# A graph layer on one core: segment sums kept in PSUM banks by TensorE, register numbers in half of the partitions, and a new split of the gather

## The chip, the cores and the metric

The kernel runs on one core of a Trainium2 chip. The metric is the device time of one execution in microseconds. A core has TensorE (PE; matmuls), VectorE (DVE), ScalarE (ACT), GpSimd (POOL) and SyncE (SP); each takes its own instructions in order, and semaphores tie them together. DMAs are issued here by SP (plain ones) and by POOL (the indirect ones, which gather rows by an index).

## The reference, cut to what matters

There are 12,500 nodes with 48 features and 400,000 edges with 32 features, sorted by their target `dst`.

```python
h = jnp.maximum(_layernorm(x, axis=-1), 0.0)
x_i, x_j = h[dst], h[src]
tmp = jnp.concatenate([x_i, x_j, edge_attr], axis=1)      # 48 + 48 + 32
h = jax.nn.relu(tmp @ W1 + b1)                            # 128 hidden
msg = h @ W2 + b2
out = x + jax.ops.segment_sum(msg, dst, num_segments=12500)
```

## The kernel before, in words

First, `node_tables` makes two tables of the nodes: A (the target's part of `W1`, with the bias) and B (the source's part), each 12,500 rows of 128 numbers in HBM. B is kept in SBUF too, turned, as `bt`: one node is one column of 128 partitions. A check of the indices then chooses between `windows` and `general`; with this data it is `windows`, and all that follows is in it.

`windows` goes over 391 chunks of 1024 edges, that is 8 tiles of 128 edges. The edges are sorted by target, so the targets of a chunk lie in a window of W = 80 nodes. For a chunk c:

- `prepare(c)` (L421): SP loads the 80 rows of table A (`rhs`), the edge features (`lhs`) and the targets (`row`). POOL gathers rows of table B, one fetch per tile of 128 edges (L442); the fetches are spread by waits on VectorE's instructions seven chunks earlier. VectorE makes two one-hot matrices: L458 (window row by edge) and L464 (`hot`, edge by window column, from `wnum`, which lies in PSUM).
- `before(c)` (L476): per tile a matmul of `lhs` with `rhs` gives the target's and the edge's part of the hidden layer in the PSUM tile `pre`.
- Not all tiles get their B rows from POOL. Some get them **by columns**: VectorE and ScalarE copy single columns of `bt`, 128x1 each, into a tile `gt` (L384), with the column's address in a register, and TensorE turns it and adds it to `pre` (`turned`, L485). A few get them **by single rows**: SP issues one DMA of 512 bytes per edge (L416).
- `gathered` (L506, L504) adds the gathered rows to `pre`, and `hidden` (L513, L515) applies the relu.
- `fold(c)`: per tile `hid` times `hot` sums the hidden rows of each node of the window (L524), and `ones` times `hot` counts its edges (L529). Both go to the PSUM tile `p_g`, 128 x 2 x 80.
- `add(c)` (L543): VectorE adds `p_g` to a segment in SBUF, at the window's place in it (an address in a register).

Segments: 12 chunks (GQ) share a segment of L = 1024 nodes. There are two segment tiles, used in turn. At a segment's end `segment_next` clears the other tile (L559, two memsets) and copies the 80 nodes that go on (L561). `segment_sum` multiplies a segment by `W2` and the counts by `b2` in two blocks of 512 columns (L569, L570), and VectorE adds each to the piece of `x` that `segment_load` fetched (L571). `segment_store` writes it to the output (L575).

Numbers for registers: the host packs, per chunk, a row of the places of columns, row numbers, window starts and so on. The rows lie in the SBUF tile `last`, chunk c in partition c % 128. `numbers` (L345; the loads carry L349) emits a load of up to 32 of them into registers of one engine. `PARTS` says which engine copies how many columns: four VectorE parts of 19, 20, 16 and 16 columns and five ScalarE parts of 16, 151 in all, so `tiles_of` makes 458 tiles by columns. SINGLE = 12 single rows per chunk make 36 tiles by rows. POOL fetches the other 2631.

The order of the work is written out by hand in the loop at the end of `windows` (L577 to L622): iteration c prepares chunk c, computes `before`, `turned`, `gathered` and `hidden` of chunk c-1, and folds and adds chunk c-2. On VectorE an iteration is: L458, columns of part 0, L464, columns of part 1, (L571), L506, columns of part 2, L513, L515, L543, (L559, L561), columns of part 3. The load of a part's numbers stands directly ahead of the part's copies, but for part 0, whose copies follow L458 and whose load lies between the two, and part 3, whose load stands ahead of L543.

Of the kernel before, what the change touches and what calls it, by code (L numbers as in the profile page):

```python
# [16 lines left out]
P = 128  # L17
# [9 lines left out]
W = 80  # L27


GQ = 12  # L30
OFF = -(NCH - 3) % GQ
L = 1024
# [3 lines left out]
BLK = 512  # L36
STORE = 2
# [18 lines left out]
    (True, 0, 19, 1),  # L56
    (True, 19, 20, 20),
    (True, 39, 16, 40),
    (True, 55, 16, 56),
    (False, 71, 16, 72),  # L60
    (False, 87, 16, 88),
    (False, 103, 16, 104),
    (False, 119, 16, 120),
    (False, 135, 16, 136),
)
PART = sum(n for _, _, n, _ in PARTS)
BASE = 152
# [3 lines left out]
SEG0 = 130848  # L71
SEG_SIZE = 8 * L


SEG, NEXT, SEG2 = 153, 154, 155
PLACE0 = 156
SINGLE = 12
SINGLE_AT = 160
WIDTH = 172
SLOTS = (NCH + 2 + P - 1) // P  # L80
MOST = 32
# [197 lines left out]
def windows(nc, tc, gp, bt, ident, idx, x_t, tab_a, tab_b, dst, edge_t, w1, w2s, b2s, out_t):  # L279
# [3 lines left out]
    with ExitStack() as es:  # L283
        seg = es.enter_context(tc.tile_pool(name="segs", bufs=1))

        segs = [seg.tile([P, 2, L], F32, name=f"seg{k}") for k in range(2)]
# [6 lines left out]
        ps_g = es.enter_context(tc.tile_pool(name="ps_g", bufs=2, space=PSUM))  # L293
        ps_f = es.enter_context(tc.tile_pool(name="ps_f", bufs=1, space=PSUM))
        xp = es.enter_context(tc.tile_pool(name="xp", bufs=2))
        ps_w = es.enter_context(tc.tile_pool(name="ps_w", bufs=1, space=PSUM))


        wnum = ps_w.tile([P, W], F32, name="wnum")
# [16 lines left out]
        place = PARTS[0][3] - 1  # L316
        for a, b in ((place, SEG2), (NEXT, SEG)):
# [4 lines left out]
        at_place = slice(place, place + 1)  # L322
        nc.vector.scalar_tensor_tensor(
            last[:, :, at_place], last[:, :, at_place], 4.0, last[:, :, PLACE0 : PLACE0 + 1],
            op0=ALU.mult, op1=ALU.add,
        )
        for seg in segs:
            nc.vector.memset(seg, 0.0)
# [16 lines left out]
        def numbers(c, at, n, engine):  # L345

            got = []
            for k in range(0, n, MOST):
                got += nc.values_load_multi_w_load_instructions(  # L349
                    last[c % P : c % P + 1, c // P, at + k : at + min(k + MOST, n)],  # L350
                    engines=[engine], min_val=0, max_val=1 << 23,
# [9 lines left out]
        def load(c, part):  # L361
# [4 lines left out]
            if part == 0 and 2 <= c < NCH + 2:  # L366
                base, *nodes = numbers(c, at - 1, n + 1, engine)
                st[c - 2]["base"] = base
            else:
                nodes = numbers(c, at, n, engine) if n else []  # L370
# [590 lines left out]
```

## Time and profile before

| | us |
|---|---|
| median of 3 runs | 3562.99 (3554.6 to 3570.09) |
| the profiled execution | 3548.53 |
| its span, first to last instruction | 3546.7 |
| mean granted TensorE clock | 0.784 of full speed |

Reading the profile: a row of a group gives line, engine, operation, output and inputs, shapes and count, then the busy time, the mean of one in ns, and the engine's idle time ahead of it with what ended it. A row of a timeline gives start, duration, engine, line, operation and tiles; neighbours of one line are merged, with their count. Instructions of one engine overlap by some tens of ns, so a group's mean duration is longer than the distance from one start to the next. DVEq, ACTq, SPq and POOLq are the sequencers of the engines: loads of registers, waits and the issue of DMAs are theirs and are not counted as busy.

### The profile page before, as it was taken

To read this page: it belongs to the slowest core of one execution; us is meant where nothing else is said; L and a number is where in the kernel's file an instruction comes from. 1 tells how busy PE (TensorE), PEld (TensorE's weight loads), DVE (VectorE), ACT (ScalarE), POOL (GpSimd) and SP (SyncE) were. 2 spreads that over 40 slices of the span, in tenths; PEclk is the share of its full clock that TensorE was granted. 3 is DMA by queue.
4 is the path that set the end of the run, shared out by engine and by line. 5 is a ranking of instruction groups with operands and counts; after the bars stand their busy time and mean duration, and the time that the engine had idled before them with its cause. 6 is when DMAs were issued, how large, how long until landed. Compare 5 with 4: busy or idle time off the path is not lost.

```text
span 3546.7 us, 119948 instructions
## 1 busy us (share of the span) xinstructions
PE 2628.1 (74%) x17111; PEld 2359.2 (67%) x17111; DVE 3258.7 (92%) x30218; ACT 3123.8 (88%) x31115; POOL 2667.2 (75%) x2658
## 2 busy tenths in 40 slices
PE   8677677777777776777777777777777777777777
PEld 6566666667666766666667666666666666666666
DVE  6799999999999999999999999999999999999997
ACT  5898989899898898988999899998988899898884
POOL 5777777777777777777777777777777777777773
PEclk9677887786777778877787778777787788777777
DMA  5533333333333333333333333333333333333332
GB/s 201 164 97 99 96 93 94 93 93 102 95 93 92 95 90 103 95 96 93 92 95 97 97 96 96 95 92 93 99 95 93 95 91 93 103 96 94 91 95 58
DMA packets 197246, 349.05 MB, mean 98 GB/s; under 512 B 67763, under 2 KB 104517, under 8 KB 195157
## 3 DMA queue, kind: packets, MB, share of 16 engines
q0 software_dynamic: 84224, 172.62, 19.2%
q1 hardware_dynamic: 111952, 168.56, 15.8%
q14 instruction: 670, 5.48, 0.5%
q8 instruction: 140, 2.29, 0.3%
q10 hardware_dynamic: 260, 0.10, 0.0%
HBM read 321.55 MB, written 22.07 MB: 97 GB/s over the span
## 4 chain that ended last, share of the span: by engine, by line
DVE 68%; PE 8%; ACT 6%; issue 5%; DVEq 4%; DMA 3%; SPq 0%; ACTq 0%; POOL 0%; POOLq 0%
DVE gt L384 38%; DVE hid L506 8%; ACT gt L384 6%; DVE hot L464 6%; DVE lhs L458 5%; DVE hid L513 5%; DVEq L349 4%; PE p_g L524 4%; DMA gb<-tab_b,srci 3%; DVE seg L543 2%; DVE hid L515 2%; PE p_f L569 1%; PE p_f L570 1%; PE pre L476 1%; PE pre L485 1%
## 5 line engine op out<-in xcount | busy, mean ns | idle before, releaser
L384 ACT COPY gt<-bt 128x1 f32 x31040 | 3077.3, 187 | 334.0 <-PE pre L485 226.2
L442 POOL DMA_INDIRECT gb<-tab_b,srci x2631 | 2645.7, 1006 | 822.5 <-issue 371.7
L384 DVE COPY gt<-bt 128x1 f32 x27584 | 1818.8, 144 | 161.1 <-issue 104.3
L524 PE MATMUL p_g<-hot,hid 128*128 128x80 f32 x6250 | 1074.6, 344 | 873.8 <-DVE hid L513 873.4
L524 PEld LDWEIGHTS p_g<-hot,hid 128*128 128x128 f32 x6250 | 1004.6, 252 | 950.1 <-DVE hid L513 940.9
L476 PEld LDWEIGHTS pre<-rhs,lhs 112*128 112x128 f32 x6250 | 964.9, 243 | 86.1 <-issue 85.2
L476 PE MATMUL pre<-rhs,lhs 112*128 112x128 f32 x6250 | 994.1, 327 | 16.5 <-DMA lhs<-in_edge_t 16.3
L506 DVE TENSOR_TENSOR hid<-pre,gb 128x896 f32<-128x896 f32 (+2 forms) x391 | 408.7, 1045 | 0.6
L464 DVE TENSOR_TENSOR hot<-wnum,rel 128x640 f32<-128x640 f32 x391 | 318.2, 814 | 0.0
L458 DVE TENSOR_SCALAR lhs<-row,bw 80x1024 f32<-80x1024 int16 x391 | 290.2, 742 | 9.2 <-DMA row<-in_dst 9.2
L485 PE MATMUL pre<-ident,gt 128*128 128x128 f32 x916 | 270.2, 403 | 9.8 <-DVE gt L384 9.6
L513 DVE TENSOR_SCALAR hid<-hid 128x896 f32<-128x896 f32 (+2 forms) x391 | 243.0, 622 | 0.1
L529 PE MATMUL p_g<-hot,ones 128*128 128x80 bf16 x3125 | 239.4, 237 | 0.0
L529 PEld LDWEIGHTS <-ones 128*128 128x128 bf16 x3125 | 239.1, 132 | 0.0
L485 PEld LDWEIGHTS pre<-ident,gt 128*128 128x128 f32 x916 | 192.4, 269 | 11.2 <-issue 11.2
L543 DVE TENSOR_TENSOR seg<-seg,p_g 128x160 f32 x391 | 124.5, 318 | 15.1 <-issue 11.4
L515 DVE TENSOR_SCALAR hid<-pre 128x128 f32<-128x128 f32 (+1 forms) x389 | 118.7, 305 | 0.0
L569 PE MATMUL p_f<-seg,w2s 128*48 128x512 f32 (+1 forms) x134 | 106.5, 890 | 0.4 <-DVE seg L543 0.4
L571 DVE TENSOR_TENSOR xseg<-xseg,p_f 48x512 f32<-48x512 f32 (+1 forms) x67 | 45.0, 672 | 50.8 <-PE p_f L570 50.7
L570 PE MATMUL p_f<-seg,b2s 1*48 1x512 f32 (+1 forms) x134 | 86.6, 731 | 0.0
L570 PEld LDWEIGHTS p_f<-seg,b2s 1*48 1x48 f32 x134 | 12.4, 135 | 87.6 <-issue 87.6
L559 DVE MEMSET seg<- 128x944 f32 x64 | 54.1, 845 | 9.3
(67 smaller groups left out, 294.7 us busy)
## 6 DMA issues: line engine op xcount, KB each, us to landing
gr<-tab_b SPq DMA_DIRECT2D x4608, 0.5 KB
row<-in_dst SPq DMA_DIRECT2D x390, 160.0 KB
lhs<-in_edge_t SPq DMA_DIRECT2D x390, 128.0 KB
gb<-tab_b,srci POOLq DMA_INDIRECT x2631
rhs<-tab_a SPq DMA_DIRECT2D x391, 40.0 KB
xseg<-in_x_t SPq DMA_DIRECT2D x33, 192.0 KB
out_x<-xseg SPq DMA_DIRECT2D x33, 192.0 KB
tab_b<-tab SPq DMA_DIRECT2D x3, 1280.0 KB
```

Source lines behind the costliest of these rows:

```text
L384: done = copy(gts[of][:, e : e + 1], bt8[:, bass.ds(at, 4)].bitcast(F32))
L442: fetch = nc.gpsimd.indirect_dma_start(out=gb[:, t, :], out_offset=None, in_=tab_b[:, :], in_offset=bass.IndirectOffsetOnAxis(ap=srci[:, c ...
L458: mark(nc.vector.tensor_scalar(lhs[:W, : n * P], row[:, : n * P], bw[:, c : c + 1], None, op0=ALU.is_equal,), 0.8)
L464: mark(nc.vector.tensor_tensor(hot[:, :n, :], wnum.unsqueeze(1).to_broadcast([P, n, W]), rel[:, c * T : c * T + n].unsqueeze(2).to_broadca ...
L476: nc.tensor.matmul(pre[:, t, :], s["lhs"][:K, t * P : (t + 1) * P], s["rhs"][:K, :], start=True, stop=t not in turned_at(c),)
L485: nc.tensor.matmul(st[c]["pre"][:, t, :], gts.pop(j), ident, start=False, stop=True)
L506: mark(nc.vector.tensor_add(to, of, rows), 1.0)
L513: mark(nc.vector.tensor_scalar(of, of, 0.0, None, op0=ALU.max), 0.55)
L515: nc.vector.tensor_scalar(apart(c, s["h"], True), apart(c, s["pre"], True), 0.0, None, op0=ALU.max)
L524: nc.tensor.matmul(p_g[:, 0, :], s["h"][:, t, :], s["hot"][:, t, :], start=t == 0, stop=t == n - 1)
L529: nc.tensor.matmul(p_g[:, 1, :], ones, high[:, t, 1::2], start=t == 0, stop=t == n - 1)
L543: mark(nc.vector.tensor_add(to, to, s["p_g"]), 0.25)
```

## The change

The segment sums stay in PSUM. A segment is now 5 chunks (GQ) and L = 432 nodes, so that its sums fill most of one bank (`sums`) and its counts part of another (`degs`); two of each are used in turn. `segment_begin` clears both with a matmul of zeros. `fold` adds straight into them, at a place that TensorE takes from two registers (two numbers per chunk, loaded by TensorE). `add` and `segment_next` are gone, and with them L543, L559 and L561 and the clearing of the segments ahead of the loop. At the next segment's start ScalarE copies the sums and the first row of the counts to SBUF (`segment_copy`); one iteration later TensorE multiplies by `W2` and `b2` back into the bank of the sums (`segment_product`); one more later VectorE copies the 80 nodes that go on from the last segment's piece of the output and adds the product (`segment_sum`). The store comes two iterations after that. `wnum` now lies in the bank of the first `degs`.

The numbers for registers lie in 64 partitions, the lower 16 of each 32 (`row_of`), and `last` is longer for it. VectorE's parts are 16, 20, 20 and 20 columns, 156 with ScalarE's, which makes 474 tiles by columns; SINGLE is 16, which makes 48 tiles by rows; POOL fetches 2603. With `add` gone, the load of part 3 stands between L515 and the copies.

```diff
-GQ = 12
+GQ = 5
-L = 1024
+L = 432
-STORE = 2
+STORE = 4
 PARTS = (
-    (True, 0, 19, 1),
-    (True, 19, 20, 20),
-    (True, 39, 16, 40),
-    (True, 55, 16, 56),
+    (True, 0, 16, 0),
+    (True, 16, 20, 16),
+    (True, 36, 20, 36),
+    (True, 56, 20, 56),
...
-SINGLE = 12
+SINGLE = 16
+HALF_ROWS = 16
+USED = P // 2
+def row_of(c):
+    group, row = divmod(c % USED, HALF_ROWS)
+    return 2 * HALF_ROWS * group + row, c // USED
...
+        sums = [ps_s.tile([P, L], F32, name=f"sum{k}") for k in range(2)]
+        beside = ps_w.tile([P, L + W], F32, name="deg0")
+        degs = [beside[:, :L], ps_w.tile([P, L], F32, name="deg1")]
+        wnum = beside[:, L:]
...
-        for seg in segs:
-            nc.vector.memset(seg, 0.0)
...
+        def segment_begin(g):
+            for of in (sums[g % 2], degs[g % 2]):
+                nc.tensor.matmul(
+                    of, zeros[:, :P], zeros, start=True, stop=False, skip_group_check=True
+                )
         def fold(c):
...
+            for at, of, first in zip(
+                numbers(c, PLACE, 2, mybir.EngineType.PE), (sums[k], degs[k]),
+                (SUM0 + k * SUM_SIZE, DEG0 + k * SUM_SIZE),
+            ):
+                at = at.with_bounds(
+                    min_val=first, max_val=first + 4 * FAR, guaranteed_mod_val=0, out_of_modulus=4
+                ) - first
+                to.append(of.bitcast(U8)[:, bass.ds(at, 4 * W)].bitcast(F32))
             for t in range(n):
                 nc.tensor.matmul(
-                    p_g[:, 0, :], s["h"][:, t, :], s["hot"][:, t, :], start=t == 0, stop=t == n - 1
+                    to[0], s["h"][:, t, :], s["hot"][:, t, :], start=False, stop=False,
+                    skip_group_check=True,
                 )
...
-            mark(nc.vector.tensor_add(to, to, s["p_g"]), 0.25)
...
+        def segment_copy(g):
+            sm[g] = segp.tile([P, 2, L], F32, name="seg")
+            nc.scalar.copy(sm[g][:, 0, :], sums[g % 2])
+            nc.scalar.copy(sm[g][:1, 1, :], degs[g % 2][:1, :])
+        def out_of(g, n):
+            return sums[g % 2][:D, :n]
+        def segment_product(g, n):
+            seg, p_f = sm.pop(g), out_of(g, n)
+            nc.tensor.matmul(p_f, w2s, seg[:, 0, :n], start=True, stop=False, skip_group_check=True)
+            nc.tensor.matmul(
+                p_f, b2s[:1, :], seg[:1, 1, :n], start=False, stop=True, skip_group_check=True
+            )
+        def segment_sum(g, n):
             if g > 0:
...
+                of, = numbers(begin(g - 1), NEXT, 1, mybir.EngineType.DVE)
+                nc.vector.tensor_copy(
+                    xs[g][:, :W],
+                    xs[g - 1][:, bass.ds(of.with_bounds(min_val=0, max_val=FAR), W)],
+                )
+            nc.vector.tensor_add(xs[g][:, :n], xs[g][:, :n], out_of(g, n))
...
+                g, k = group(c - 2)
                 if 0 <= c - 2 < NCH:
+                    if c - 2 == begin(g):
+                        segment_begin(g)
                     fold(c - 2)
                 if 0 <= c - 1 < NCH:
                     turned(c - 1)
+                if g > 0 and k == 1:
+                    segment_product(g - 1, L)
+                if g > 0 and k == 2:
+                    segment_sum(g - 1, L)
                 if k == GQ - 3 or c == NCH - 1:
                     segment_load(g)
-                if g > 0 and k < L // BLK:
-                    segment_sum(g - 1, k, BLK)
                 if g > 0 and k == STORE:
                     segment_store(g - 1, L)
...
                 load(c, 3)
-                if 0 <= c - 2 < NCH:
-                    add(c - 2)
-                    if k == GQ - 1:
-                        segment_next(g)
                 columns(c, 3)
                 for part in range(DVE_PARTS, len(PARTS)):
                     load(c, part)
                     columns(c, part)
+                    if g > 0 and k == 0 and part == DVE_PARTS:
+                        segment_copy(g - 1)
```

More of the change, by code (lines that the diff above doesn't have):

```diff
@@ L365, in load @@
             engine = mybir.EngineType.DVE if dve else mybir.EngineType.Activation
[L366 to L370, printed above, removed]
-            regs[c, part] = nodes
+            regs[c, part] = numbers(c, at, n, engine) if n else []
         def columns(c, part):
@@ L907 @@
     by_tile = src.reshape(NT, P)
-    numbers = np.zeros((SLOTS * P, WIDTH), np.int32)
+    numbers = np.zeros((LAST * USED, WIDTH), np.int32)
     first = dst[::CE]
```

106 lines of the change are left out of this document (45 added, 61 removed).

## The prediction

> **What bounds the kernel now.** I read the page first, then the view of one line (L458, once per chunk), then the timeline of VectorE over one chunk, then SyncE's queue.
>
> ```profile
> PE 2628.1 (74%) x17111; PEld 2359.2 (67%) x17111; DVE 3258.7 (92%) x30218; ACT 3123.8 (88%) x31115; POOL 2667.2 (75%) x2658
> ...
> L384 ACT COPY gt<-bt 128x1 f32 x31040 | 3077.3, 187 | 334.0 <-PE pre L485 226.2
> L442 POOL DMA_INDIRECT gb<-tab_b,srci x2631 | 2645.7, 1006 | 822.5 <-issue 371.7
> L384 DVE COPY gt<-bt 128x1 f32 x27584 | 1818.8, 144 | 161.1 <-issue 104.3
> ```
>
> VectorE is the fullest. But POOL's 75% is a full engine as well: (2645.7 + 822.5) / 2631 = 1.32 us from fetch to fetch, and most of the idle part is 0.3 us of "issue" ahead of each. The next row gives the period.
>
> ```profile
> L458 DVE TENSOR_SCALAR lhs<-row,bw x391: 535/740/927, 104.4 to 3524.8; 80x1024 f32<-80x1024 int16 x195, 80x640 f32<-80x640 int16 x1
> ```
>
> (3524.8 - 104.4) / 390 = 8.77 us per chunk. One plain chunk on VectorE (timeline; start, us, engine, line), and three of its sequencer's loads of register numbers (one line's view; duration, then start):
>
> ```profile
> 2085.44 0.74 DVE L458 TENSOR_SCALAR lhs<-row,bw 80x1024 f32<-80x1024 int16 x1
> 2086.58 1.25 DVE L384 COPY gt<-bt 128x1 f32 x19 [0.40 <-issue]
> 2087.74 0.82 DVE L464 TENSOR_TENSOR hot<-wnum,rel 128x640 f32<-128x640 f32 x1
> 2088.64 1.31 DVE L384 COPY gt<-bt 128x1 f32 x20
> 2089.86 1.08 DVE L506 TENSOR_TENSOR hid<-pre,gb 128x896 f32<-128x896 f32 x1
> 2090.86 1.05 DVE L384 COPY gt<-bt 128x1 f32 x16
> 2091.83 0.61 DVE L513 TENSOR_SCALAR hid<-hid 128x896 f32<-128x896 f32 x1
> ...
> 2092.57 0.32 DVE L543 TENSOR_TENSOR seg<-seg,p_g 128x160 f32 x1
> 2092.80 1.05 DVE L384 COPY gt<-bt 128x1 f32 x16
> 2093.78 0.74 DVE L458 TENSOR_SCALAR lhs<-row,bw 80x1024 f32<-80x1024 int16 x1
> ```
>
> ```profile
> L349 DVEq TENSOR_LOAD <-last x1: 1101/1101/1101, 2089.6 to 2089.6; - x1
> L349 DVEq TENSOR_LOAD <-last x1: 1098/1098/1098, 2091.4 to 2091.4; - x1
> L349 DVEq TENSOR_LOAD <-last x1: 1348/1348/1348, 2093.2 to 2093.2; - x1
> ```
>
> Two things to see. A copy costs (2089.86 - 2088.64) / 20 = 0.061 us. And a load of 16 numbers takes 1.10 us, one of 20 numbers 1.35, so 0.062 us per number; the copies behind it start some 0.1 us after it has ended. It begins some 0.2 to 0.6 us ahead of the long operation in front of it (2093.2 against 2093.78, 2089.6 against 2089.86, 2091.4 against 2091.83), because the sequencer runs that far ahead, and it is free only as far as that operation covers it. The two loads of 20 stick out (after L458 and L464), the two of 16 just fit.
>
> **The change, VectorE.** (a) Five more copies: 5 x 0.061 = +0.31 us per chunk. (b) The load behind L458 falls from 20 numbers to 16: begun 0.55 us ahead, it ends 0.55 us after L458's start, under L458 itself. The first copy then comes 0.66 us after L458's start (0.74 less the overlap of 0.08 between neighbours, as in 2092.57 + 0.32 against 2092.80) instead of about 0.9, as after L464 here (1.14 after L458 in this chunk): -0.25. (c) The load behind L506 grows to 20: 2089.6 + 1.35 is 2090.95, the copies start near 2091.08 instead of 2090.86: +0.22. (d) L543 goes, 0.23 us. But the load behind L515 grows to 20 as well and has lost L543 as cover: 2091.4 + 1.35, and 0.1 to start, is 2092.8, where the copies start now. So the add's gain is eaten: 0. (e) Numbers in the lower 16 of each 32 partitions. The two rows are 8 chunks whose numbers lie in the lower half and 8 in the upper:
>
> ```profile
> L349 DVEq TENSOR_LOAD <-last x33: 1097/1346/1373, 2068.2 to 2134.8; - x33
> L349 DVEq TENSOR_LOAD <-last x33: 1122/1380/1395, 2489.8 to 2557.7; - x33
> ```
>
> 25 to 34 ns a load; three loads show, in half of the chunks: 0.03 x 3 / 2 = -0.05. Sum of (a) to (e): +0.23 us per plain chunk.
>
> A rule speaks against (b) to (d): the Trainium skill (DMA: Bandwidth & Descriptors, Latency and other measured facts) gives a register load a floor of about 600 ns, as if its size did not matter. By that, (c) and (d) would cost nothing. The rows above disagree: 16 and 20 numbers differ by 0.25 us.
>
> (f) The segment work. Now, every 12 chunks:
>
> ```profile
> 1942.88 0.32 DVE L543 TENSOR_TENSOR seg<-seg,p_g 128x160 f32 x1
> 1943.35 1.83 DVE L559 MEMSET seg<- 128x944 f32 x2
> 1945.10 0.18 DVE L561 COPY seg<-seg 128x160 f32 x1
> 1945.19 1.05 DVE L384 COPY gt<-bt 128x1 f32 x16
> ...
> 1950.38 0.67 DVE L571 TENSOR_TENSOR xseg<-xseg,p_f 48x512 f32<-48x512 f32 x1
> ```
>
> ```profile
> DVE xseg L571 <- PE p_f L570: 50.7, 36, 3.9
> ```
>
> From L543 to the copies 2.31 us instead of 0.23, two adds of 0.6, and 50.7 / 33 = 1.5 of waiting for the product: 4.8 us, 0.40 per chunk. Afterwards, every 5 chunks: a copy of 48x80 (at most the 0.18 above), an add of 432 columns (432/512 x 0.67 = 0.57), and one more register load, mostly under queued copies. That is 0.75 / 5 = 0.15. The product now stands one chunk ahead of its add, so its wait goes, though a late TensorE can delay L506 instead (third rival). Saving: 0.25.
>
> VectorE alone: +0.23 - 0.25, about -0.02 us per chunk, with 0.1 of doubt either way: no change. The two memsets ahead of the loop (L328) are 3.5 us that I leave in the doubt.
>
> **ScalarE and POOL.** ScalarE gets two copies of 432 columns per segment, of which there are 79: about 0.57 us each by L571's price, so 90 us in all. It stood idle for 334.0 us, and runs ahead: covered. POOL has 2603 fetches instead of 2631 (474 tiles by columns instead of 458, 48 by rows instead of 36): 28 x 1.32 = 37 us less, not on the path unless the others get faster.
>
> **SyncE, the term that decides.** It issues one 512-byte row per DMA, 12 a chunk now, 16 afterwards. Its timeline in a stretch where it waits for nothing, then one with a segment load, then its load of 12 numbers, and its first and last issue:
>
> ```profile
> 1871.69 0.32 SPq L427 DMA_DIRECT2D rhs<-tab_a  x1
> ...
> 1880.73 3.86 SPq L416 DMA_DIRECT2D gr<-tab_b  x12
> 1885.35 0.32 SPq L427 DMA_DIRECT2D rhs<-tab_a  x1
> ...
> 1892.62 0.32 SPq L427 DMA_DIRECT2D rhs<-tab_a  x1
> ```
>
> ```profile
> 1902.66 3.87 SPq L416 DMA_DIRECT2D gr<-tab_b  x12
> ...
> 1908.11 0.32 SPq L427 DMA_DIRECT2D rhs<-tab_a  x1
> ```
>
> ```profile
> L349 SPq TENSOR_LOAD <-last x1: 777/777/777, 1909.4 to 1909.4; - x1
> ```
>
> ```profile
> L427 SPq DMA_DIRECT2D rhs<-tab_a x391: 322/322/342, 94.9 to 3505.7; - x196
> ```
>
> Three chunks in 1892.62 - 1871.69 = 20.93 us: 6.98 each, against a period of 8.77, so SyncE has room today (it issues its last rhs 19 us ahead of the last L458). Four more rows at (3.86 - 0.23) / 11 = 0.33: +1.32. Four more numbers at VectorE's price of 0.062 (a load of 12 is 0.777, which is 0.065 each): +0.25. That is 8.55. A segment load costs (1908.11 - 1906.53) - (1885.35 - 1884.59) = 0.82; a store, whose issue I have no clean row for, I take at 1.0. The pair comes every 5 chunks instead of 12: 1.82 / 5 = 0.36. So **8.91 us per chunk of pure issuing, above the 8.77 of today**. Bounds: without hiccups two chunks take (1885.35 - 1871.69) / 2 = 6.83 each; with 1.28 for the rows, 0.2 for the numbers and 0.36 that is 8.67. With rows at 0.34 and a dearer store (0.45) it is 9.04.
>
> **Sum.** SyncE issues singles up to iteration 384. It reaches that one at 94.9 + 384 x 8.91 = 3516, and L458 follows some 4 us later (estimate: the row of destinations is the third DMA, and has to land): 3520. VectorE needs 6 more plain chunks of about 8.5, 51 us, and from the last L458 to the end 3546.7 - 3524.8 = 22: 3593, against 3546.7. With the 1.8 us around the span, 3595 against its own 3548.5, a factor of 1.013. The profiled execution lies 0.4% under the median of 3562.99, so I forecast 3610.
>
> **Rivals.**
> *SyncE just keeps up* (its 8.67): VectorE decides, 8.70 to 8.85 us: -27 to +31 us, about 3535 to 3595 on the median's scale, centred on no change. For it: the add and the memsets really go. Against it: one of the three chunks shown has a hiccup of 0.4 us (7.27 instead of 6.83). 0.26.
> *Faster*: the loads of (c) and (d) begin earlier than today and hide, and (d)'s 0.23 is won: VectorE at 8.3. Then the next to be late are SyncE at 8.67, which by the sum above ends at 94.9 + 384 x 8.67 + 77 = 3501, and POOL, whose fetches alone take 2603 x 1.32 = 3436 us behind the tables. About 3505 to 3530. For it: the sequencer's run ahead varies. Against it: it is shortest (0.2 us) ahead of L506. 0.11.
> *TensorE late in half clock.* Here is a chunk in half clock, with the two VectorE operations around it:
>
> ```profile
> 1909.17 3.70 PE L524 MATMUL p_g<-hot,hid 128*128 128x80 f32 x16 [4.05 <-DVE hid L513]
> 1912.66 0.74 PE L529 MATMUL p_g<-hot,ones 128*128 128x80 bf16 x8
> 1913.20 0.78 PE L485 MATMUL pre<-ident,gt 128*128 128x128 f32 x2
> ...
> 1917.70 0.56 PE L524 MATMUL p_g<-hot,hid 128*128 128x80 f32 x3 [0.32 <-DVE hid L513]
> ```
>
> ```profile
> 1912.56 0.81 DVE L464 TENSOR_TENSOR hot<-wnum,rel 128x640 f32<-128x640 f32 x1
> ...
> 1914.81 1.09 DVE L506 TENSOR_TENSOR hid<-pre,gb 128x896 f32<-128x896 f32 x1
> ```
>
> TensorE's 8.53 us fill that chunk, and L506 follows L485 by 0.83. The change adds to it two registers per chunk and 24 matmuls whose destination is in a register (by VectorE's load of 2 numbers, 0.2 us; below nothing there is no way), and two zeroing matmuls per segment. wnum now shares a bank with the counts of every second segment, so L529 may have to wait for L464's end at 1913.37, 0.7 late. Each 1 us more in that place is 0.2 to 1 us of waiting in half-clock chunks, some 0.4 of all: 390 x 0.4 x 0.5 = 78 us on top, about 3650 to 3690. 0.13.
> The Trainium skill (PSUM — Partial Sum Buffer, PSUM bank collisions raise a hardware error) says that two engines must be kept apart by bank, not by address. By that, the wait for L464 is there; no run so far shows it.
> That the half of the partitions does nothing is worth 0.05 x 390 = 18 us on VectorE, nothing where SyncE decides.
>
> **Numbers.** SyncE decides: 0.50. A difference under 0.5% (3545 to 3581) is about what cannot be told from no change. The case in which SyncE keeps up is split: half of it the same, a quarter to each side. Slower: 0.50 + 0.13 + 0.07 = 0.70. Same: 0.13. Faster: 0.11 + 0.06 = 0.17. The range 3520 to 3675 leaves out the fast end and the worst of TensorE.
>
> **What would show it.** Right: SyncE's rhs issued only a few us ahead of its L458, no waits at L427, L458 waiting for the row's DMA, a period near 8.9. The copies after L506 and L515 show idle time put down to issue, those after L458 none. Wrong: SyncE still 15 to 20 us ahead, or a period under 8.7, or L506 waiting for L485.

## The result and the profile after

The changed kernel takes 3839.58 us (median of 4 runs, 3827.97 to 3846.04) against 3558.80 (4 runs, 3547.61 to 3570.09) on the same chip: a ratio of 1.0785 with a 95% interval of 1.0741 to 1.0830. It is slower, as forecast, but by 281 us and not by some 50, and outside the range of 3520 to 3675. The profiled execution took 3840.84 us, its span is 3839.1, the mean granted clock 0.727 (before: 0.784).

All later experiments but j1 to j3 ran on chips on which the kernel before itself takes 4413 to 4484 us, so a time is compared only with the kernel before, or another kernel, of the same job (kernels run one after another on one chip).

The page of the changed kernel, engine sums and the largest groups:

```profile
PE 2859.4 (74%) x17349; PEld 2522.9 (66%) x17349; DVE 3272.3 (85%) x31811; ACT 3191.9 (83%) x31341; POOL 2629.8 (69%) x2631
...
L447 POOL DMA_INDIRECT gb<-tab_b,srci x2603 | 2607.9, 1002 | 1071.3 <-issue 431.4
L389 ACT COPY gt<-bt 128x1 f32 x31108 | 3076.3, 187 | 89.3 <-issue 66.2
L389 DVE COPY gt<-bt 128x1 f32 x29564 | 1943.7, 144 | 300.0 <-issue 247.7
...
L511 DVE TENSOR_TENSOR hid<-pre,gb 128x896 f32<-128x896 f32 (+2 forms) x391 | 405.9, 1038 | 185.6 <-PE pre L490 172.4
...
L568 ACT COPY seg<-deg 1x432 f32<-1x432 f32 x79 | 39.9, 505 | 397.7 <-DVE hot L469 325.5
...
L527 PE MATMUL deg<-zeros 1*128 1x432 bf16 x79 | 39.2, 496 | 274.9 <-DVE hot L469 274.9
```

Line numbers have moved: L389 was L384 (the copies), L447 L442 (POOL's fetches), L511 L506 (the gathered part added to `pre`), L469 L464 (hot), L463 L458 (lhs). No engine is fuller than before. VectorE's work grew by 13.6 us while the span grew by 292; the rest is waiting. Part of it stands ahead of L511: 172.4 us for L490, the last thing that TensorE writes into `pre`. On TensorE a new row waits longer still: the matmul of zeros that clears the counts, 274.9 us for hot. ScalarE's copy of the counts (L568) waits too, 325.5 us for hot, but that did not reach the path: L490, which takes ScalarE's columns, has no idle time ahead of it (0.0 us).

The view of the one line L463 gives the period; the list of waits gives the pattern (engine, tile and line, what it waited for: total us, times, longest):

```profile
L463 DVE TENSOR_SCALAR lhs<-row,bw x391: 539/740/945, 105.4 to 3818.1; 80x1024 f32<-80x1024 int16 x195, 80x640 f32<-80x640 int16 x1
```

```profile
PE deg L527 <- DVE hot L469: 274.9, 40, 8.4
PE deg L551 <- DVE hot L469: 224.4, 118, 2.6
```

(3818.1 - 105.4) / 390 = 9.52 us a chunk, against 8.77. L527 clears the counts once in a segment, 79 times, and it waited 40 times: in every second segment. That is the pattern of `wnum`, which lies beside the counts of every second segment, and which L469 reads. The starts of L463 for the chunks 20 to 387, sorted by place in the segment and by the bank of its counts, show the same in the period (mean us from one L463 to the next, 36 or 37 chunks each):

| chunk of the segment | counts share wnum's bank | counts in the other bank |
|---|---|---|
| 1st | 13.02 | 8.84 |
| 2nd | 8.91 | 8.69 |
| 3rd (add of the segment's sum) | 10.54 | 9.99 |
| 4th | 9.06 | 8.85 |
| 5th | 8.82 | 8.70 |
| mean | 10.07 | 9.01 |

Here is one first chunk of the first column, TensorE and VectorE in its timeline (start, us, engine, line):

```profile
1907.36 0.42 DVE L520 TENSOR_SCALAR hid<-pre 128x256 f32<-128x256 f32 x1
...
1909.08 0.74 DVE L463 TENSOR_SCALAR lhs<-row,bw 80x1024 f32<-80x1024 int16 x1
...
1910.73 0.81 DVE L469 TENSOR_TENSOR hot<-deg,rel 128x640 f32<-128x640 f32 x1
...
1911.59 0.51 PE L527 MATMUL deg<-zeros 1*128 1x432 bf16 x1 [7.80 <-DVE hot L469]
1912.09 1.30 DVE L389 COPY gt<-bt 128x1 f32 x20 [0.55 <-issue]
...
1912.20 3.67 PE L545 MATMUL sum<-hot,hid 128*128 128x80 f32 x16
...
1915.66 0.74 PE L551 MATMUL deg<-hot,ones 128*128 128x80 bf16 x8
...
1916.20 0.78 PE L490 MATMUL pre<-ident,gt 128*128 128x128 f32 x2
...
1917.01 1.09 DVE L511 TENSOR_TENSOR hid<-pre,gb 128x896 f32<-128x896 f32 x1 [3.61 <-PE pre L490]
...
1921.90 0.74 DVE L463 TENSOR_SCALAR lhs<-row,bw 80x1024 f32<-80x1024 int16 x1
```

Even the input is named `deg` in L469's row: the numbers of columns and the counts are one tile. TensorE is idle from 1903.8 on (7.80 us ahead of L527). The fold (L545) needs only the hot and hidden parts of the chunk before, and the last of these, L520, ended at 1907.8. But L527 stands ahead of it in TensorE's queue, and L527 may not write that bank before L469 has read it, at 1911.54. Only then do the 16 sum matmuls, the 8 count matmuls and L490 run, 5.4 us in a row, and VectorE, which could have started L511 at 1913.4, waits 3.61 us. The next L463 comes at 1921.90, 12.82 us after this one. Part of the 5.4 us is the clock: the granted clock is 0.50 from 1912 to 1917, and 16 of L545 take 3.67 us there, against 2.01 us at 1957.87, at a granted clock of 1.00. The held folds of segments 4 to 77 all ran so, 37 of 37, and of the first folds of the other segments 24 of 37. The trace agrees with the rule that the prediction quoted from the Trainium skill (PSUM — Partial Sum Buffer, the section on collisions): the accesses of two engines were kept apart by bank, though the columns differ.

What the two columns differ by is (10.07 - 9.01) / 2 = 0.53 us a chunk, 206 us of the 292 (below, this is called the reckoning by position); that it is the price of the shared bank has to be tried. The other 9.01 - 8.77 = 0.24, some 90 us, comes on every segment.

VectorE in a plain chunk, and around the add of a segment's sum:

```profile
2280.05 0.74 DVE L463 TENSOR_SCALAR lhs<-row,bw 80x1024 f32<-80x1024 int16 x1
2280.71 1.05 DVE L389 COPY gt<-bt 128x1 f32 x16
2281.68 0.81 DVE L469 TENSOR_TENSOR hot<-deg,rel 128x640 f32<-128x640 f32 x1
2282.65 1.31 DVE L389 COPY gt<-bt 128x1 f32 x20 [0.16 <-issue]
2283.87 1.08 DVE L511 TENSOR_TENSOR hid<-pre,gb 128x896 f32<-128x896 f32 x1
2285.08 1.30 DVE L389 COPY gt<-bt 128x1 f32 x20
2286.30 0.62 DVE L518 TENSOR_SCALAR hid<-hid 128x896 f32<-128x896 f32 x1
2286.83 0.28 DVE L520 TENSOR_SCALAR hid<-pre 128x128 f32<-128x128 f32 x1
2287.25 1.54 DVE L389 COPY gt<-bt 128x1 f32 x20
2288.71 0.74 DVE L463 TENSOR_SCALAR lhs<-row,bw 80x1024 f32<-80x1024 int16 x1
```

```profile
2600.02 1.30 DVE L389 COPY gt<-bt 128x1 f32 x20 [0.16 <-issue]
2601.68 0.37 DVE L584 COPY xseg<-xseg 48x80 f32 x1 [0.35 <-issue]
2602.15 0.59 DVE L588 TENSOR_TENSOR xseg<-xseg,sum 48x432 f32<-48x432 f32 x1
2602.92 0.96 DVE L511 TENSOR_TENSOR hid<-pre,gb 128x768 f32<-128x768 f32 x1 [0.18 <-PE pre L490]
2604.60 1.30 DVE L389 COPY gt<-bt 128x1 f32 x20 [0.72 <-issue]
```

The plain chunk is the predicted one: 0.66 us from L463 to its copies (2280.71 - 2280.05), 1.21 from L511 to its copies, and 8.66 in all. The segment's chunk is not: ahead of L584 a register has to be loaded (0.35 idle), and the load behind L511 now begins later too (0.72 idle, none in the plain chunk).

SyncE, which the forecast put on the path, waits and stays far ahead:

```profile
L432 SPq DMA_DIRECT2D rhs<-tab_a x391: 322/322/958, 95.3 to 3796.5; - x196
```

```profile
SPq L432 <- PE pre L481: 260.4, 87, 7.1
```

Its last rhs is issued 3818.1 - 3796.5 = 21.6 us ahead of the last L463. Without its waits at L432 it needs 8.87 us a chunk (chunks 20 to 380: 9.519 x 360 us, less 232 of waiting for L481); without the short waits at its other lines as well, 53 us in all, 8.73.

### The profile page after: what moved, and what is told of

It reads as the page before. It is cut to its first block, busy times and chain, and to the rows that moved or that the text cites. A ratio compares the mean times of both kernels' runs of the same rounds, so it can differ in the third digit from the quotient of the medians.

```text
span 3839.1 us, 126111 instructions
## 1 busy us (share of the span) xinstructions
PE 2859.4 (74%) x17349; PEld 2522.9 (66%) x17349; DVE 3272.3 (85%) x31811; ACT 3191.9 (83%) x31341; POOL 2629.8 (69%) x2631
## 4 chain that ended last, share of the span: by engine, by line
DVE 62%; PE 14%; issue 9%; DVEq 5%; DMA 5%; POOL 3%; ACT 1%; SPq 1%; ACTq 0%; POOLq 0%
DVE gt L389 37%; DVE hid L511 7%; DVE hot L469 6%; PE sum L545 5%; DVE lhs L463 5%; DVEq L359 5%; DVE hid L518 5%; DMA gb<-tab_b,srci 4%; POOL gb L447 3%; DVE hid L520 2%; PE pre L481 2%; PE pre L490 2%; PE deg L551 1%; PE p_n L235 1%; ACT gt L389 1%
## 5 line engine op out<-in xcount | busy, mean ns | idle before, releaser
L447 POOL DMA_INDIRECT gb<-tab_b,srci x2603 | 2607.9, 1002 | 1071.3 <-issue 431.4
L389 ACT COPY gt<-bt 128x1 f32 x31108 | 3076.3, 187 | 89.3 <-issue 66.2
L389 DVE COPY gt<-bt 128x1 f32 x29564 | 1943.7, 144 | 300.0 <-issue 247.7
L545 PEld LDWEIGHTS sum<-hot,hid 128*128 128x128 f32 x6250 | 1016.8, 255 | 816.6 <-DVE hid L518 497.9
L545 PE MATMUL sum<-hot,hid 128*128 128x80 f32 x6250 | 1078.7, 345 | 435.5 <-DVE hid L518 431.2
L481 PEld LDWEIGHTS pre<-rhs,lhs 112*128 112x128 f32 x6250 | 1082.7, 269 | 98.9 <-issue 97.7
L481 PE MATMUL pre<-rhs,lhs 112*128 112x128 f32 x6250 | 1112.1, 353 | 17.5 <-DMA gr<-tab_b 17.1
L511 DVE TENSOR_TENSOR hid<-pre,gb 128x896 f32<-128x896 f32 (+2 forms) x391 | 405.9, 1038 | 185.6 <-PE pre L490 172.4
L551 PE MATMUL deg<-hot,ones 128*128 128x80 bf16 x3125 | 248.1, 244 | 230.7 <-DVE hot L469 224.4
L551 PEld LDWEIGHTS <-ones 128*128 128x128 bf16 x3125 | 248.0, 135 | 248.5 <-issue 248.5
L568 ACT COPY seg<-deg 1x432 f32<-1x432 f32 x79 | 39.9, 505 | 397.7 <-DVE hot L469 325.5
L469 DVE TENSOR_TENSOR hot<-deg,rel 128x640 f32<-128x640 f32 x391 | 317.4, 812 | 0.0
L463 DVE TENSOR_SCALAR lhs<-row,bw 80x1024 f32<-80x1024 int16 x391 | 290.0, 742 | 14.5 <-DMA row<-in_dst 14.5
L490 PE MATMUL pre<-ident,gt 128*128 128x128 f32 x948 | 292.9, 423 | 0.0
L527 PE MATMUL deg<-zeros 1*128 1x432 bf16 x79 | 39.2, 496 | 274.9 <-DVE hot L469 274.9
L490 PEld LDWEIGHTS pre<-ident,gt 128*128 128x128 f32 x948 | 211.4, 286 | 0.0
L567 ACT COPY seg<-sum 128x432 f32<-128x432 f32 x79 | 40.5, 513 | 111.0 <-PE sum L545 93.8
L520 DVE TENSOR_SCALAR hid<-pre 128x128 f32<-128x128 f32 (+1 forms) x389 | 121.1, 311 | 0.0
L576 PE MATMUL sum<-seg,w2s 128*48 128x432 f32 (+1 forms) x158 | 106.0, 765 | 0.4 <-ACT seg L567 0.4
L577 PE MATMUL sum<-seg,b2s 1*48 1x432 f32 (+1 forms) x158 | 102.2, 737 | 0.0
```

The lines of the kernel that those rows point to most:

```text
L389: done = copy(gts[of][:, e : e + 1], bt8[:, bass.ds(at, 4)].bitcast(F32))
L447: fetch = nc.gpsimd.indirect_dma_start(out=gb[:, t, :], out_offset=None, in_=tab_b[:, :], in_offset=bass.IndirectOffsetOnAxis(ap=srci[:, c ...
L463: mark(nc.vector.tensor_scalar(lhs[:W, : n * P], row[:, : n * P], bw[:, c : c + 1], None, op0=ALU.is_equal,), 0.8)
L469: mark(nc.vector.tensor_tensor(hot[:, :n, :], wnum.unsqueeze(1).to_broadcast([P, n, W]), rel[:, c * T : c * T + n].unsqueeze(2).to_broadca ...
L481: nc.tensor.matmul(pre[:, t, :], s["lhs"][:K, t * P : (t + 1) * P], s["rhs"][:K, :], start=True, stop=t not in turned_at(c),)
L490: nc.tensor.matmul(st[c]["pre"][:, t, :], gts.pop(j), ident, start=False, stop=True)
```

## Experiments

Theory A: the bank that `wnum` shares with the counts of every second segment costs the 206 us, through the queue of TensorE. B: TensorE's own new work or its lower clock. C: SyncE's sixteen rows. The first two experiments undo A in two ways.

**The other bank** (e1, and again as f1, g1, h2 and k2). The numbers of columns are kept twice, beside both counts; each chunk's hot reads the copy beside the counts that TensorE does not fill:

```diff
-        beside = ps_w.tile([P, L + W], F32, name="deg0")
-        degs = [beside[:, :L], ps_w.tile([P, L], F32, name="deg1")]
-        wnum = beside[:, L:]
+        beside = [ps_w.tile([P, L + W], F32, name=f"deg{k}") for k in range(2)]
+        degs = [of[:, :L] for of in beside]
+        wnums = [of[:, L:] for of in beside]
...
-                hot[:, :n, :], wnum.unsqueeze(1).to_broadcast([P, n, W]),
+                hot[:, :n, :], wnums[(group(c - 2)[0] + 1) % 2].unsqueeze(1).to_broadcast([P, n, W]),
```

> The change with one edit: wnum is kept twice, beside the counts of both segments, and L469 reads the copy whose bank the running segment does not write. Theory A (bank): the counts' zeroing matmul waits for L469 because wnum shares its bank, and the whole fold stands behind it in TensorE's queue. The chunks of segments with a bank of their own take 9.01 us in the changed kernel's trace, those with the shared bank 10.07; all should now take 9.01, a span of 3839 - 0.53 x 391 = 3633 us, ratio to before 1.024. Theory B (TensorE's new work, its lower granted clock of 0.727, register addresses): the time stays within 1% of 3839. Theory C (SyncE with 16 rows decides, 8.88 us net of waits): no lower than about 3600.

**The late zero** (e2, again as f2 and k4). The bank stays shared, but the zeroing of the counts moves behind the sum matmuls in TensorE's queue:

```diff
-            for of in (sums[g % 2], degs[g % 2]):
+            for of in (sums[g % 2],):
...
+            if c == begin(group(c)[0]):
+                nc.tensor.matmul(
+                    degs[k], zeros[:, :P], zeros, start=True, stop=False, skip_group_check=True
+                )
             high = s["hot"].bitcast(BF16)
```

> The change with wnum left in the counts' bank, but the zeroing matmul of the counts issued behind the fold's sum matmuls instead of ahead of them. Theory A in its narrow form (what costs is that the waiting matmul stands ahead of the fold): the first chunk of every second segment falls from 13.0 to about 9.2 us, 149 us in all, a span near 3690; the rest of the 206 us stays. If the shared bank costs by any wait for L469, wherever it stands, the gain is under 60 us. Theory B: no change from 3839.

**Twelve rows** (e3): the other bank, and `SINGLE = 12` (with `WIDTH = 176`, since four fewer numbers are stored).

> As the first kernel, and SyncE issues 12 rows a chunk as before instead of 16 (36 tiles by rows, 12 more fetches on POOL). Theory C (SyncE decides once the bank is out of the way): faster than the first kernel by 0.5% or more, SyncE's net period near 7.5 us. If VectorE decides (plain chunks of 8.70 us and 1.3 us more in the chunk of the segment's sum): within 0.3% of the first kernel, about 3633.

**Upper half** (e4): the other bank, and the numbers in the upper 16 of each 32 partitions: `2 * HALF_ROWS * group + HALF_ROWS + row`.

> As the first kernel, but the numbers for registers lie in the upper 16 of each 32 partitions. If the load of numbers is what sticks out behind L469, L511 and L520 and reads the upper half 25 to 34 ns slower: three loads x 0.03 x 391 = 35 us slower than the first kernel, about 1%, the VectorE loads of 20 numbers at 1.38 us instead of 1.35. If SyncE decides, or the half does nothing: within 0.3% of the first kernel.

Measured in one job, where the kernel before took 4414.35: e1 4414.03 (ratio 1.0001, 0.9986 to 1.0016), e2 4415.56 (one run), e3 4399.02 (0.9971, 0.9957 to 0.9985), e4 4418.61 (1.0012, 0.9996 to 1.0027). None of the times expected came, because the kernel before was 24% slower too; without the changed kernel beside them they don't size the bank. What the traces could still say: the first chunks of the two kinds of segment took 10.77 and 10.81 us in e1, 10.89 and 10.78 in e2. The difference of 4.2 us is gone in both. Two small terms can be read against e1: four rows fewer save 15 us (0.34%, between the two answers named ahead), and the upper half costs 4.6, which the intervals don't tell from nothing. The loads themselves do differ by the half: VectorE's loads of 20 numbers take 1.387 us in e4 against 1.354 in e1, those of 16 take 1.131 against 1.105 (medians).

**Both again** (f1, f2 in one job, g1 in another), for other conditions.

> The change with wnum kept twice, L469 reading the copy in the bank that the running segment does not write; once more, since on the chip of the first attempt the kernel before itself took 4414 us. Where the kernel before takes about 3560: theory A (the shared bank) expects 3633 us, ratio 1.024; theory B (TensorE's new work) 3839, ratio 1.078; theory C (SyncE's 16 rows) not under 3600. Where the kernel before takes about 4414 again, all take the same, whatever the theory.

> The change with the counts' zeroing matmul behind the fold's sum matmuls. On a chip where the kernel before takes about 3560: theory A in its narrow form expects near 3690 us, the first chunk of every second segment at 9.2 us instead of 13.0; a gain under 60 us would mean that any wait for L469 costs, wherever it stands; theory B expects 3839.

> A third look at the change with wnum kept twice, beside the kernel before, to see what a chip does on which VectorE's and ScalarE's copies do not stall. With the kernel before at about 3560: theory A 3633 us, theory B 3839, theory C not under 3600. With the kernel before at 4400 or more: the same as it.

Measured: f1 4482.40 and f2 4483.13 (one run) against 4483.93, g1 4426.81 against 4427.31 (one run each). The same again, as expected for such a chip, and no size.

**The changed kernel itself beside the other bank, one with fewer columns, and the kernel before** (h1, h2, h3, h4). h3 is the other bank with

```diff
-    (True, 0, 16, 0),
-    (True, 16, 20, 16),
-    (True, 36, 20, 36),
-    (True, 56, 20, 56),
+    (True, 0, 18, 0),
+    (True, 18, 18, 18),
+    (True, 36, 18, 36),
+    (True, 54, 18, 54),
...
-SINGLE = 16
+SINGLE = 14
...
-WIDTH = 180
+WIDTH = 174
```

> The changed kernel itself, unaltered, beside the next kernels on one chip. If the kernel before takes near 3560 us here: 3839 again, ratio 1.075 to 1.083, and the first chunk of every second segment near 13 us against 8.8 in the others. If the kernel before takes 4410 to 4490 here, as on the chips of the earlier experiments, theory D (there the half-microsecond stalls of VectorE and ScalarE set the period, and all else is hidden) expects a ratio of 0.998 to 1.02: the shared bank's wait for L469 is still in the trace, but less of it reaches VectorE; theory A (the shared bank's wait is added to whatever the period is) expects 1.04 to 1.05, some 200 us more.

> The changed kernel with the numbers of columns kept beside both counts, each chunk's hot reading the copy in the bank that TensorE does not fill. If the kernel before takes near 3560 us here: theory A (shared bank) expects 3615 to 3650, 206 us below the changed kernel, which is the even segments' excess over the odd ones; theory B (TensorE's own new work) 3800 to 3840; theory C (SyncE's sixteen rows) 3800 to 3840. If the kernel before takes 4410 to 4490: 1.00 again.

> The kernel of the other bank, and VectorE's four parts of 18 columns each (72 in place of 76), 14 single rows on SyncE in place of 16, POOL fetching the rest (about 18 fetches more, 24 us of POOL's time). If the kernel before takes near 3560 us here: VectorE loses four columns of 0.061 us and what of their loads is not hidden, 0.24 to 0.5 us a chunk, SyncE 0.66 us; the period goes from 9.0 to about 8.5 to 8.75, and the time to 3500 to 3560, POOL's own 3505 the floor. If the stalls of 0.5 us set the period (4410 to 4490 for the kernel before): four copies of 76 fewer on VectorE, 0 to 3 per cent below the kernel before.

> The kernel before, unaltered, for a trace of it on the same chip. If it takes near 3560 us: the trace known already. If 4410 to 4490: theory D expects VectorE's copies to stand 0.085 to 0.09 us apart with stalls of about 0.5 us in number and sum as in the changed kernel (700 to 900 us), and VectorE to wait for no other engine.

Measured against 4413.37: h1 4512.93 (1.0224, 1.0189 to 1.0258), h2 4410.35 (0.9992, 0.9976 to 1.0009), h3 6971.55 (1.58), h4 4405.21 (one run). Now the two kernels stand side by side, and they differ by where the numbers of columns lie alone: 4512.93 - 4410.35 = 102.6 us. TensorE's new work and SyncE's rows are the same in both, so neither is the cause of this part; and h2's VectorE hardly waits for TensorE at all. The granted clock was 0.683 in h2 and 0.669 in h1; that the clock is not the cause is seen below, where the late zero is as fast at 0.650. The sorted periods of h1 are 13.43 us for the first chunk of a sharing segment and 10.74 for that of the others, and the means of the two kinds of segment differ by 11.43 - 10.87, or 0.55 before rounding; half of it, times 390, is 108 us. The reckoning by position agrees with the run to 6%. In h1's trace VectorE waited for L490, and in h2's list of VectorE's waits that row is gone:

```profile
DVE gt L389 <- issue: 785.0, 1827, 1.9
DVE hid L511 <- PE pre L490: 133.9, 44, 5.9
```

```profile
DVE gt L390 <- issue: 804.9, 1902, 1.4
DVE lhs L464 <- issue: 26.4, 33, 12.4
```

Of the theories named ahead for such a job, A (1.04 to 1.05) is too high. D (0.998 to 1.02: stalls set the period and hide most of the wait) is just short of 1.0224, but the interval reaches into its range. The first rows show what is different there: copies of VectorE stand still for about half a microsecond with no releaser, 785 us in all (247.7 in the changed kernel's first trace). The kernel before has it too (h4; the prediction's page has 104.3 us in 3546.7):

```profile
DVE gt L384 <- issue: 679.2, 1640, 3.7
...
ACT gt L384 <- issue: 859.0, 2262, 4.3
```

(The two rows are from two lists, VectorE's and ScalarE's waits.) A plain chunk of VectorE lasts 10.6 to 10.8 us there instead of 8.7. That the wait for the bank costs less than 206 us because it hides behind these stalls is likely, but not shown.

h3 came out 58% slower, where up to 3% faster was expected. Its register loads show why. ScalarE's loads of 16 numbers, in two stretches of the same run (count, min/median/max ns, first and last start):

```profile
L360 ACTq TENSOR_LOAD <-last x5: 1021/1023/1028, 999.1 to 1005.4; - x5
```

```profile
L360 ACTq TENSOR_LOAD <-last x3: 3480/3482/3482, 2288.9 to 2297.0; - x3
```

A row of 174 numbers is 696 bytes, 8 more than a multiple of 16, so the rows of every second slot begin 8 bytes off (a slot is one of the places for rows in a partition; 64 chunks in a row use the same one). On VectorE, where parts begin at 0, 18, 36 and 54 numbers, loads of 18 take 1.57 and 4.07 us (medians), one as often as the other. Even the faster is dearer than the 1.35 us of 20 numbers, so the count seems to matter too; no run tries that alone. So h3 tells nothing of fewer columns. It tells that the place of a row counts, and j1 tries that alone.

**The pitch, and few columns with and without the shared bank** (j1, j2, j3). j1 is the other bank with `WIDTH = 182`. j2 is the other bank with eight parts of 16 columns, four on each engine (64 and 64 instead of 76 and 80); j3 has the same eight parts and the shared bank of the changed kernel.

> The kernel of the other bank, with nothing changed but the pitch of the table of numbers: 182 numbers a row in place of 180, so that in every second slot of the table the rows begin at 8 bytes past a multiple of 16. If the place of the numbers made the kernel of fewer columns slow (its ScalarE loads of 16 numbers took 1.02 us in one slot and 3.48 us in the next): in three of the seven slots the loads of 16 take about 3.5 us and those of 20 about 4.3 us, in the other four 1.02 and 1.35 as before, and the time is between 5500 and 6500 us; if its fewer columns or 14 rows did it: the time of the other-bank kernel again, 4350 to 4500.

> The kernel of the other bank with 64 columns on VectorE (four parts of 16, every part aligned) in place of 76, and 64 on ScalarE (four parts of 16) in place of 80; POOL fetches the rest, about 85 fetches more. Where the kernel before takes 4400 to 4490 us: VectorE's chunk of 10.99 us loses 12 copies of 0.088 us and up to three 0.25 us of loads, ScalarE's 16 copies of 0.125 us; period 9.2 to 9.9, time 3730 to 4010, ratio 0.84 to 0.91. Where it takes near 3560: POOL is the bound (2690 fetches of 1.31 us and 64 us), 3580 to 3640.

> The same columns as the kernel just before it, but the numbers of columns in the one bank, as in the changed kernel. Theory A (the shared bank holds the zeroing, the fold behind it and then VectorE's gathered part): less work of VectorE lies between the hot part and the gathered part to hide it, so that the price is above the 103 us that it was with 76 columns on such a chip and at most the 206 us of the first traces: 105 to 210 us above the kernel just before it, all of it in the first chunk of every second segment, 2.7 to 5 us longer than the others. Theory B (TensorE's new work itself): no difference, within 20 us.

These three ran on a chip on which the kernel before takes 3556.28. Measured: j1 5939.36 (one run), j2 3585.25 (1.0087, 1.0069 to 1.0105), j3 3591.71 (1.0097, 1.0080 to 1.0114).

j1 changes one number and comes out as expected: ScalarE's loads of 16 take 3.49 us in one slot and 1.02 in the next, and the copies wait.

```profile
L360 ACTq TENSOR_LOAD <-last x2: 3494/3494/3495, 999.7 to 1003.9; - x2
```

```profile
L360 ACTq TENSOR_LOAD <-last x13: 1020/1022/1064, 2500.5 to 2519.8; - x13
```

The changed kernel itself has every load of 16 or 20 numbers at a multiple of 16 bytes (its parts begin at 0, 16, 36, 56 and so on, a row is 720 bytes), so this is no part of its loss.

j2's time is in the range given, but not by the engine that was named, POOL. Its SyncE issues the last rhs 3558.2 - 3535.5 = 22.7 us ahead of the last L463, which is after the single rows have ended; in the chunks 20 to 380 it is 3.4 to 5.1 us ahead, waits at most 0.7 us at a time (35 us in all), and sets the period of 8.86. VectorE shows it by its waits for the row of destinations:

```profile
L432 SPq DMA_DIRECT2D rhs<-tab_a x391: 322/322/1149, 96.6 to 3535.5; - x196
```

```profile
DVE lhs L463 <- DMA row<-in_dst: 233.9, 274, 2.5
```

This is the state that the forecast described, with its signs: sixteen rows on SyncE do cost 8.86 us a chunk, and they bind as soon as VectorE is quicker. And with SyncE as the bound, the shared bank costs next to nothing: j3 - j2 is 6.5 us, with intervals that overlap, where A expected 105 to 210. The wait is there (first chunks of sharing segments 12.54 us, VectorE waits 232.5 us for L489, its L490), but several of the others run at 7.8, which is less than SyncE's 8.86, because SyncE had got ahead in the long chunk (it is 3.5 to 9.6 us ahead there):

```profile
DVE hid L510 <- PE pre L489: 232.5, 117, 5.5
```

The other bank has a side effect, which is off the path in j2, where SyncE decides: hot now reads, in every segment, the bank from which ScalarE copies the counts, and that copy (L568) waits 815.4 us for hot in all.

The reckoning by position would give (9.21 - 8.59) / 2 x 390 = 122 us here. The run gave 6.5. The reckoning holds only where VectorE works without a pause in the other chunks as well; otherwise they give the time back.

**At the changed kernel's own columns, all four beside each other** (k1 the changed kernel, k2 the other bank, k4 the late zero; k3 the other bank with parts of 16, 20, 20 and 16 columns, `SINGLE = 12` and `WIDTH = 172`, so that every load is at a multiple of 16 bytes).

> The changed kernel itself, beside the next three on one chip. Where the kernel before takes near 3560 us: 3839 again, 1.074 to 1.083, the first chunk of every second segment near 13.0 us and of the others near 8.8. Where it takes 4400 to 4490: 1.019 to 1.026 again.

> The changed kernel with the numbers of columns kept beside both counts. Where the kernel before takes near 3560 us: theory A (shared bank) 3615 to 3650, 190 to 225 us below the changed kernel, with the first chunks of all segments near 8.8 us; theories B (TensorE's new work) and C (SyncE's sixteen rows) within 40 us of the changed kernel. What is left above the kernel before, 60 to 90 us, theory A puts on VectorE's five more columns, its loads of 20 and the segment's sum in one chunk. Where the kernel before takes 4400 to 4490: 1.00 again.

> The kernel of the other bank with VectorE's parts of 16, 20, 20 and 16 columns (72 in place of 76, each load at a multiple of 16 bytes), and 12 single rows on SyncE in place of 16; POOL fetches 24 times more. Where the kernel before takes near 3560 us: VectorE's chunk of 9.01 us loses four copies of 0.061 us and a load's 0.25 us, 8.5 us, so 3440 to 3480 by VectorE alone, and POOL, which took 3585 us for 2688 fetches, would take about 3510 for 2627; time 3500 to 3560. Where the kernel before takes 4400 to 4490: four copies of 0.088 us and a load's 0.25 us fewer, 4200 to 4380.

> The changed kernel with the one shared bank left as it is, but the counts' zeroing matmul issued behind the 16 sum matmuls of the fold, so that what waits for the hot part no longer holds them. Where the kernel before takes near 3560 us: if it is the order in TensorE's queue that costs (theory A as refined), 3630 to 3700, at least 140 us below the changed kernel, the first chunks of even segments within 0.8 us of the odd; if the bank's wait itself costs wherever it stands, 3800 to 3840. Where the kernel before takes 4400 to 4490: 1.00 again.

Measured against 4479.23: k1 4581.82 (1.0233, 1.0212 to 1.0255), k2 4475.57 (0.9990, 0.9978 to 1.0002), k3 4478.42 (1.0000, 0.9990 to 1.0009), k4 4486.75 (1.0018, 1.0007 to 1.0029). The bank costs 4581.82 - 4475.57 = 106 us (105 by position). The late zero, which leaves the bank shared, gets 95 of the 106 back, at a granted clock of 0.650 against 0.662 in k1: it is the place in TensorE's queue that cost, and not the clock. A wait for hot that stands behind the sums is cheap: k4's count matmuls (L555) still wait 199.3 us for it in all. In k4's page the zeroing hardly waits and L511 is on time:

```profile
L511 DVE TENSOR_TENSOR hid<-pre,gb 128x896 f32<-128x896 f32 (+2 forms) x391 | 405.8, 1038 | 48.6 <-PE pre L490 18.8
...
L550 PE MATMUL deg<-zeros 1*128 1x432 bf16 x79 | 39.6, 501 | 55.0 <-DVE hot L469 42.6
```

k3 was expected at 4200 to 4380 and changed nothing. ScalarE's 80 copies a chunk, with their stalls, fill the time there, which would explain that four fewer on VectorE gain nothing:

```profile
L390 ACT COPY gt<-bt 128x1 f32 x31040 | 3257.1, 187 | 987.2 <-issue 930.1
```

3257.1 + 987.2 is 95% of its span of 4469.7, and of the idle part at most 57 us is a wait for another engine. So k3 does not tell whether the remaining 90 us of the changed kernel are VectorE's columns. No version beat the kernel before by 0.5%; e3, with twelve rows, came nearest at 0.9971.

## Why the prediction was wrong

**VectorE's plain chunk: right within 0.1.** 8.77 less the 0.40 of segment work is 8.37, and (a) to (e) add 0.23: 8.60. The chunks without segment work (second and fifth, other bank) take 8.70. The loads behind L463 and L511 hid and showed as the rows of before had it.

**SyncE: the size right, the place wrong.** 8.91 us a chunk was forecast as pure issuing; 8.86 is the period in j2, where SyncE decides and the time is 3585. (Net of every wait it needs 8.73 in the changed kernel, so the sum was 0.18 too high by its own terms.) In the changed kernel it never came to that: at 9.52 us a chunk SyncE has time to spare. The forecast's 0.50 for "SyncE decides" went to a state that did not come.

**Segment work: too cheap.** (f) put 0.75 us on the chunk with the add; in segments that do not share the bank it is 9.99 - 8.70 = 1.29, since the copy and its register load show, and the run ahead that hides the next load is lost. With 0.15 on two other chunks, that is 0.31 us a chunk (9.01 - 8.70) instead of 0.15; most of the saving that was to pay for (a) to (d) did not come. Forecast were 8.75 us a chunk for VectorE alone; 9.01 came, 0.10 of the difference from the plain chunk and 0.16 from here. That makes the 0.24 us a chunk, some 90 us, by which every segment is above the kernel before. It is read from the trace alone; no run separates it.

**TensorE late: the step that failed.** The sum that gave 3610 had no term for TensorE; it put the wait for the shared bank at nothing, and only a rival priced it. The rival saw that `wnum` shares a bank with the counts of every second segment, and said that "L529 may have to wait for L464's end at 1913.37, 0.7 late", worth part of 78 us, at a chance of 0.13. L529's successor L551 does wait so, 224.4 us in 118 times. But the change adds another writer of that bank, the zeroing matmul, and `segment_begin` issues it ahead of the fold. There the wait holds not 8 matmuls at the end but all 24 and L490 behind them: 4.2 us in the first chunk of every second segment, 0.42 a chunk, and with the smaller waits 0.53, so 206 us for the 78. The prediction listed "two zeroing matmuls per segment" without a price, and did not ask what each waits for and what is queued behind it. (Its 0.2 us for a load of two numbers comes from no row; TensorE's loads of two took 0.54 us, the median in the changed kernel.) That the bank is the cause is shown by two pairs that differ in nothing else (102.6 and 106 us), that it is the queue by the late zero (95 of 106). The 206 us itself is a reckoning by position. It met these two pairs within 6% and missed j2 and j3, where SyncE was the bound, by far (122 against 6.5); for the changed kernel's own columns it was not measured where the kernel before takes 3560 us. There, 3839.6 - 206 = 3634 would be left. That lies within the range given, but partly by luck: VectorE, at 9.01 us a chunk, would set it, and not SyncE, as the forecast had it.

**Half of the partitions:** the prediction's 18 us is for half of the chunks; with all of them in the upper half, as in e4, it would be 35. The loads grew as forecast, by 26 and 33 ns, but the time only by 4.6 us, on a chip where VectorE and ScalarE stall in between. What it is worth where VectorE's loads decide stays open.

## What to carry to other kernels

Ask of each new instruction not only what it takes but what it waits for, and what stands behind it in its engine's queue; a matmul of half a microsecond that waits for a bank can hold five microseconds of work that was ready. Small constants that another engine reads don't belong in a bank that TensorE accumulates into, or the first write to it belongs behind the work that doesn't need it. A price read from one stage's long chunks holds only while nothing else, here SyncE's queue, lets the short chunks give it back.

## What the runs showed of the hardware that was not expected

- A register load depends on its address. 16 numbers take 1.02 us on ScalarE from a multiple of 16 bytes, 3.48 from 8 bytes past it (h3, j1); on VectorE 18 numbers take 1.57 and 4.07 (h3). One change of a row's pitch, from 180 to 182 numbers, made a kernel take 5939 us.
- TensorE's 24 matmuls whose destination comes from registers cost no more than others: 16 of L545 take 3.67 us at a granted clock of 0.50, where 16 of L524 took 3.70.
- Where the kernel before takes 4413 to 4484 us, VectorE and ScalarE stop for about half a microsecond at a time in the middle of their copies, 679 and 859 us in h4 against 104 and 62 before, with the loads of registers as short as elsewhere. What causes that was not found.
